# FFN input transposed by DMA, doubled scales spread by two DMAs, quantizing in place: one change to a planned four-stage kernel

## The chip, the cores and the metric

The kernel runs on one core of one Trainium2 chip. A core has TensorE (PE in the profile, its weight loads are PEld), VectorE (DVE), ScalarE (ACT), GpSimd (POOL) and SyncE (SP), which here only issues DMAs. Matmuls write to PSUM, eight banks of 128 x 512 floats; everything else lies in SBUF, 128 partitions wide. The metric is the device time of one execution in microseconds, given as the median of several runs.

## The reference

The input x is [4, 2048, 256], float32. Four residual stages follow each other; each normalizes x with a layer norm and adds its result to x.

```python
x = L0_attn_a_x
x = x + _L0_attn_a_ref(_layernorm(x, axis=-1), ...)
x = x + _L0_ffn_ref(_layernorm(x, axis=-1), w_gate, w_up, w_down)
x = x + _L0_attn_b_ref(_layernorm(x, axis=-1), ...)
x = x + _L0_ffn_ref(_layernorm(x, axis=-1), w_gate, w_up, w_down)
```

The first attention has a factor s / s, which it computes, and values v. The second is a linear attention over the first axis of x, which has 4 entries, with 16 heads of 16 and two gates. What the change touches is the FFN, which runs twice with the same weights. Its linear layers take both operands through a 4-bit grid, in blocks of 16 along the last axis:

```python
def fp4_quant_dequant(x):
    xb = x.reshape(shape[:-1] + (shape[-1] // BLOCK, BLOCK))
    scale = jnp.max(jnp.abs(xb), axis=-1, keepdims=True) / 6.0
    scale = jnp.maximum(scale, jnp.float32(1e-12))
    xn = xb / scale
    idx = jnp.searchsorted(_MID, jnp.abs(xn))
    q = _GRID[idx] * jnp.sign(xn) * scale
    return q.reshape(shape)

gate = fp4_linear(x, w_gate)      # x: 256 wide, w_gate and w_up: [704, 256]
y = fp4_linear(x, w_up)
h = jax.nn.silu(gate) * y
return fp4_linear(h, w_down)      # w_down: [256, 704]
```

So both the normalized input (256 wide, 16 blocks a row) and the hidden h (704 wide, 44 blocks a row) are put on the grid, one scale a block. For a matmul the contracted axis must lie on the partitions, so both have to be transposed.

## The kernel before

The rows of x are cut into 16 groups (`group(j)`) of 128 positions on the second axis times all 4 entries of the first (S = 4). A group is one tile x of [128, 4, 256], which stays in SBUF through all four stages: `attention_a`, `ffn_in` and four `ffn_tile` for k = 1, `attention_b`, and `ffn_in` and four `ffn_tile` for k = 2. That makes 32 inputs (`ffn_in`) and 128 hidden tiles (`ffn_tile`), of which the last four, of the last group in the second FFN, go a way of their own (`apart` is false). Before the groups, `first_pass` takes sums over the whole of x, and loads the weights and puts them on the grid (`quantize`, eight pieces).

Nothing is issued by hand in a loop's order. Every step is entered with `op(engine, us, rank, fn, reads, writes, ...)`: an engine, an assumed duration, a rank, and the buffers that it reads and writes. `land` is the time that a DMA is assumed to take after its issue, `port` marks steps that VectorE and GpSimd may not do at the same time, and `spare` says how many buffers of a pool must be left. `Plan.order` then plays the steps through with these costs: on each engine it takes the ready step with the lowest rank whose buffers are to be had. The program is written in the order that comes out. The ranks are offsets of a step in its stage plus the stage's begin, and the begins stand in the table `BEGIN`: one row a group, six numbers for attention a, the first input, its tiles, attention b, the second input, its tiles. Buffers come from pools of a few tiles each (`tiles(name, n, shape, ...)`); a step that needs one waits until the last user of one is done. Each engine, and SyncE's queue of DMAs, works strictly in the order written.

The path of one input (`ffn_in`):

1. GpSimd computes the reciprocal root of the variance (`root`), ScalarE normalizes four slices of x into xn (L384). Its blocks are 17 wide, the 17th element holds a small floor.
2. `to_grid`: VectorE takes the largest magnitude of each block (L1215) and its reciprocal (L1225) into the three rows of sx, divides by the scales into qax (L390); ScalarE takes magnitudes times 2^22 into qmx, in bfloat16 (L396); VectorE adds the larger of that and a floor (L403) and subtracts it again (L406), which rounds to the grid's steps. qax then holds the grid values, in float32.
3. `times_scales`: ScalarE divides the maxima by 6 (L1270), GpSimd multiplies qax by the scales (L1278).
4. `turn`: TensorE transposes qax in two banks of four 128 x 128 pieces (L1152), ScalarE copies each bank into one of six tiles of the pool turned (L1159).

The path of one hidden tile (`ffn_tile`): TensorE multiplies turned with gate and up weights in two halves (L1455), ScalarE takes the silu (L1476), VectorE the product h (L1487). `to_grid` follows, with h, qa, qm and sh as buffers, but its last pass writes grid values in bfloat16 to qm (128 x 768, the last 64 columns are zero). `scales_turned` transposes the 44 maxima of each row on TensorE (L1294), ScalarE divides by 6 into sT (L1302), and six DMAs, one for each chunk of 128 hidden features, write each scale's row 16 times to the partitions of its block, in the tile hqT (L1311): DMAs of 128 x 128, the last of 64 x 128. One DMA transposes qm to gT in six blocks (L1513). GpSimd multiplies hqT by gT (L1522), and TensorE multiplies with the down weights (L1559). VectorE adds to x (L342 or L1591). In the second FFN a DMA stores the rows (L1599).

The four tiles that are not apart take the way of the input: scales by `times_scales` on qa, transposes by TensorE (L1535), copies by ScalarE (L1548).

The other stages' matmuls are all in `project` (L1175), their transposes in `turn` too.

Of the kernel before, what the change touches and what calls it, by code (L numbers as in the profile page):

```python
# [14 lines left out]
ALU = mybir.AluOpType  # L15
# [241 lines left out]
def kernel(  # L257
# [79 lines left out]
    dev = one([P, D], "dev")  # L337
# [50 lines left out]
    def over_scales(a, src, rs):  # L388

        nc.vector.scalar_tensor_tensor(  # L390
            blocks(a), over_blocks(rs), -6.0 * BELOW, src, ALU.mult, ALU.mult
        )
# [30 lines left out]
    floored = tiles("xn", 1, [P, S * D // BLK, BLK + 1], fp)  # L423
    floored += tiles("h", 3, [P, FB, BLK + 1], fp)
    tiles("qax", 2, [P, S * D], fp)
    tiles("qmx", 1, [P, S * D], fp, BF16)
    tiles("sx", 2, [P, 3, S * D // BLK], fp)
    tiles("sil", 2, [P, HF], fp)
    tiles("qa", 3, [P, FF], fp)
# [5 lines left out]
    tiles("sT", 2, [FB, P], fp)  # L435
    tiles("sh", 4, [P, 3, FB], fp)
# [17 lines left out]
    def first_pass():  # L454
# [264 lines left out]
        def quantize(at, load, p, n):  # L719
            raw, a, m, w = (plan.buf(t) for t in ("hqT", "qa", "qm", "sh"))  # L720
# [6 lines left out]
            def sc(i):  # L727
                return w.ap[:p, i, :g]
# [22 lines left out]
                lambda: over_scales(ap(a), blocks(ap(raw)), sc(2)),  # L751
                [(raw, 0), (w, 0)],
                [(a, 0)],
# [6 lines left out]
                lambda: to_steps(ap(m), ap(a)),  # L760
                [(a, 0)],
                [(m, 0)],
            )
            for i, step in enumerate((to_sum, from_sum)):
# [4 lines left out]
                    lambda step=step: step(ap(a), ap(m)),  # L769
                    [(m, 0)],  # L770
                    [(a, 0)],
# [7 lines left out]
                    blocks(ap(a)), blocks(ap(a)), over_blocks(sc(1))  # L779
                ),  # L780
                [(w, 1)],
                [(a, 0)],
                port=True,
            )
            return a
# [3 lines left out]
        for i, chunks in enumerate(((0, 1), (2, 5), (6, 7), (3, 8), (4, 9), (10,))):  # L789
# [16 lines left out]
            def turn(a=a, tp=tp, n=n):  # L806
                for c in range(KC):
                    for t in range(n):
                        nc.tensor.transpose(
                            tp.ap[:, (n * c + t) * P : (n * c + t + 1) * P],  # L810
                            a.ap[:, t * D + c * P : t * D + (c + 1) * P],
# [15 lines left out]
        for i in range(2):  # L827
# [7 lines left out]
            for h in range(2):  # L835
                tp = plan.buf("bank")

                def turn(a=a, tp=tp, h=h):
                    for c in range(3):
# [3 lines left out]
                            tp.ap[:n, c * P : (c + 1) * P], a.ap[:, f : f + n], ident  # L843
# [131 lines left out]
        squares = plan.buf("qa")  # L975
# [133 lines left out]
        (-378, -314, -1376, -1348, 17, -996),  # L1109
        (-171, 99, -285, -130, -472, 322),  # L1110
        (122, 38, -748, 219, 388, -82),
        (158, 551, 236, -943, -736, 79),
        (122, 249, 41, 366, 26, 456),
        (302, -212, 210, 483, 172, 520),
        (311, -49, 469, 567, 672, 628),
        (524, -460, -821, 668, 512, 748),
        (519, 272, 567, 701, -1142, 842),
        (-796, 432, 635, -1, 85, -733),
        (591, 210, 709, 812, 491, 900),
        (587, -818, 708, 347, -832, 1075),  # L1120
        (669, 869, 776, 998, 617, 372),
        (704, 918, 497, 497, 654, 1040),
        (878, -478, 120, -465, -5, 1514),
        (799, 1104, 439, 1042, 488, 420),
    ]

    def group(j):
# [79 lines left out]
        def to_grid(at, src, parts, a, m, q, us, to=None):  # L1207

            v = blocks_of(src)
            n = us["n"]  # L1210
# [5 lines left out]
                    q.ap[:, 0, :], src.ap, AX.X, ALU.max, apply_absolute_value=True  # L1216
                ),
                [(src, i) for i in parts],
# [6 lines left out]
                lambda: nc.vector.reciprocal(q.ap[:, 2, :], q.ap[:, 0, :]),  # L1225
# [7 lines left out]
                lambda: over_scales(a.ap, v(), q.ap[:, 2, :]),  # L1233
                [(src, i) for i in parts] + [(q, 2)],
                [(a, 0)],
# [6 lines left out]
                lambda: to_steps(m.ap[:, :n], a.ap),  # L1242
                [(a, 0)],
# [6 lines left out]
                lambda: to_sum(a.ap, m.ap[:, :n]),  # L1250
                [(m, 0)],
                [(a, 0)],
# [5 lines left out]
                at + 4.1,  # L1258
                lambda: from_sum(a.ap, m.ap[:, :n], to and to.ap[:, :n]),
                [(a, 0), (m, 0)],  # L1260
                [(to or a, 0)],
                port=True,
            )

# [52 lines left out]
        def blocks_of(b):  # L1317
            return lambda: b.ap[:, :, :BLK]
# [575 lines left out]
```

## Time and profile before

| | |
|---|---|
| median of 3 runs | 1483.82 us (1482.01 to 1486.37) |
| the profiled execution's own time | 1483.54 us |
| its span, first to last instruction | 1481.7 us |
| TensorE, idle in the span | 44.9 us |
| VectorE, idle in the span | 137.7 us |
| ScalarE, GpSimd busy | 794.4, 769.7 us |
| DMA queue of SyncE | 220880 packets, 95.60 MB, 33.8% of 16 engines' span |
| mean clock granted to TensorE | 0.998 |

A row of the profile's groups reads: source line, engine, operation, output <- inputs (numbers of buffers left out), shapes, how many; then busy time in us and the mean of one in ns; then the idle time of the engine just before these instructions and what ended it. A row of waits reads: who waited <- for whom, us in total, times, longest. A row of the timeline reads: start, length in us, engine, line, operation, how many of them are put together, and in brackets the idle time before. SPq is SyncE's queue, where the length of a DMA is the time of its issue and not of its transfer. PE's matmuls overlap each other, so that the durations of single ones add up to more than the busy time.

### The profile page before, as it was taken

How to read it: one execution, taken by the hardware profiler on the slowest of the kernel's cores; microseconds unless marked ns; L12 is line 12 of the kernel's file. 1: busy time of each engine (PE TensorE's matmuls, PEld its weight loads, DVE VectorE, ACT ScalarE, POOL GpSimd, SP SyncE). 2: the span in 40 equal slices, each digit the busy share in tenths (PEclk: the TensorE clock that was granted, in tenths of full speed). 3: DMA queues.
4: the chain of work that ended last, by engine and by line, in shares of the span. 5: the costliest groups of instructions: out<-in, count | busy, mean ns of one | idle time of the engine just before them, and what ended most of it. 6: DMA issues, size and time to landing. Idle time of an engine off the chain costs nothing.

```text
span 1481.7 us, 19959 instructions
## 1 busy us (share of the span) xinstructions
PE 1436.8 (97%) x5742; PEld 998.8 (67%) x5742; DVE 1344.0 (91%) x2139; ACT 794.4 (54%) x1693; POOL 769.7 (52%) x787
## 2 busy tenths in 40 slices
PE   7989999999999999999999999999999999999998
PEld 6745667666767667676666666676677667676776
DVE  6799999999899999988997999988999898999995
ACT  6656557742674545544376455557525744546332
POOL 5344556534763646454644537556365654564532
PEclk9999999999999999999999999999999999999999
DMA  8402422124324334143432433231344134322451
GB/s 258 120 0 37 65 44 38 35 51 81 61 45 83 65 63 79 36 86 55 89 74 34 65 58 68 46 67 27 60 96 78 38 62 74 63 56 40 92 90 40
DMA packets 220990, 96.87 MB, mean 65 GB/s; under 512 B 108240, under 2 KB 220624, under 8 KB 220880
## 3 DMA queue, kind: packets, MB, share of 16 engines
q1 hardware_dynamic: 220880, 95.60, 33.8%
q8 instruction: 45, 0.74, 0.2%
q14 instruction: 65, 0.53, 0.1%
HBM read 18.09 MB, written 8.39 MB: 18 GB/s over the span
## 4 chain that ended last, share of the span: by engine, by line
PE 67%; DVE 13%; POOL 7%; DMA 5%; issue 4%; ACT 3%; SPq 1%; POOLq 0%; ACTq 0%; DVEq 0%
PE bank L1455 30%; PE bank L1175 17%; PE bank L1559 17%; PE bank L1152 3%; DMA gT<-qm 3%; POOL hqT L1522 2%; DVE qa L403 1%; DVE qm L406 1%; DVE pp L1666 1%; DVE h L1487 1%; DVE sh L1215 1%; DVE qa L390 1%; DVE x L342 1%; POOL norms_f L358 1%; PE bank L1294 1%
## 5 line engine op out<-in xcount | busy, mean ns | idle before, releaser
L1455 PE MATMUL bank<-wguT,turned 128*128 128x352 f32 x2048 | 634.2, 459 | 2.0 <-ACT sil L1476 2.0
L1455 PEld LDWEIGHTS bank<-wguT,turned 128*128 128x128 f32 x2048 | 380.4, 190 | 201.5 <-issue 11.8
L1522 POOL TENSOR_TENSOR hqT<-hqT,gT 128x768 f32<-128x768 f32 x124 | 228.8, 1849 | 258.6 <-DMA gT<-qm 117.4
L1559 PE MATMUL bank<-wdT,hqT 128*128 128x256 f32 x1536 | 350.9, 380 | 7.1 <-POOL hqT L1522 6.6
L1559 PEld LDWEIGHTS bank<-wdT,hqT 128*128 128x128 f32 x1536 | 288.7, 190 | 66.8 <-POOL hqT L1522 16.7
L1476 ACT ACTIVATE sil<-bank 128x352 f32<-128x352 f32 x256 | 115.7, 457 | 131.5 <-PE bank L1455 123.3
L396 ACT ACTIVATE qm<-qa 128x704 bf16<-128x704 f32 (+2 forms) x136 | 106.0, 780 | 96.9 <-DVE qa L390 74.6
L1487 DVE TENSOR_TENSOR h<-sil,bank 128x352 f32<-128x352 f32 x256 | 128.4, 506 | 29.6 <-ACT sil L1476 15.5
L1774 POOL TENSOR_TENSOR pp<-vg,sc 128x1024 f32<-128x1024 f32 x64 | 138.6, 2179 | 22.2 <-DVE tok L1795 20.1
L403 DVE SCALAR_TENSOR_TENSOR qa<-qm,qa 128x704 f32<-128x704 bf16 (+2 forms) x136 | 141.0, 1039 | 7.7 <-ACT qm L396 7.4
L390 DVE SCALAR_TENSOR_TENSOR qa<-sh,h 128x704 f32<-128x704 f32 x128 | 133.4, 1047 | 0.5
L406 DVE SCALAR_TENSOR_TENSOR qm<-qm,qa 128x704 bf16<-128x704 bf16 x124 | 126.8, 1025 | 0.2
L1175 PE MATMUL bank<-wvz,turned 128*128 128x512 f32 x256 | 119.8, 608 | 6.9 <-ACT turned L1159 3.5
L1175 PE MATMUL bank<-wqkB,turned 128*128 128x512 f32 x256 | 120.4, 593 | 1.8 <-ACT turned L1159 1.8
L1159 ACT COPY turned<-bank 128x512 f32<-128x512 f32 x160 | 87.5, 584 | 64.2 <-PE bank L1152 63.8
L1215 DVE TENSOR_REDUCE sh<-h 128x44 f32<-128x748 f32 x128 | 118.3, 924 | 2.0
L1278 POOL TENSOR_TENSOR qax<-qax,sx 128x1024 f32<-128x1024 f32 x32 | 68.1, 2128 | 90.2 <-DVE qax L406 73.8
L348 ACT ACTIVATE dev<-x,norms_f 128x256 f32<-128x256 f32 x128 | 64.7, 506 | 50.5 <-DVE x L342 48.1
L1175 PEld LDWEIGHTS bank<-wvz,turned 128*128 128x128 f32 x256 | 47.6, 193 | 56.9 <-issue 42.5
L1666 DVE TENSOR_TENSOR pp<-qk 128x1024 f32<-128x1024 f32 x64 | 83.2, 1312 | 0.6 <-ACT qk L1654 0.6
L1302 ACT ACTIVATE sT<-bank 44x128 f32<-44x128 f32 x124 | 32.8, 267 | 92.7 <-PE bank L1294 50.8
L384 ACT ACTIVATE xn<-x,norms_f 128x256 f32<-128x256 f32 x128 | 67.5, 593 | 21.3 <-POOL norms_f L378 18.2
(193 smaller groups left out, 2079.3 us busy)
## 6 DMA issues: line engine op xcount, KB each, us to landing
hqT<-sT SPq DMA_DIRECT2D x620, 64.0 KB
x<-in_L_attn_a_x_dram SPq DMA_DIRECT2D x23, 512.0 KB
out_dram<-x SPq DMA_DIRECT2D x64, 128.0 KB
hqT<-sT SPq DMA_DIRECT2D x124, 32.0 KB
gT<-qm SPq DMA_TRANSPOSE x124
hqT<-in_L_ffn_w_down_dram SPq DMA_DIRECT2D x2, 352.0 KB
hqT<-in_L_ffn_w_gate_dram SPq DMA_DIRECT2D x5, 128.0 KB
hqT<-in_L_ffn_w_up_dram SPq DMA_DIRECT2D x5, 128.0 KB
```

The lines of the kernel that those rows point to most:

```text
L390: nc.vector.scalar_tensor_tensor(blocks(a), over_blocks(rs), -6.0 * BELOW, src, ALU.mult, ALU.mult)
L396: nc.scalar.activation(m, a, AF.Abs, scale=UP)
L403: nc.vector.scalar_tensor_tensor(a, m, FLOOR, a, ALU.max, ALU.add)
L406: nc.vector.scalar_tensor_tensor(a if to is None else to, m, FLOOR, a, ALU.max, ALU.subtract)
L1175: nc.tensor.matmul(bank.ap[:, :n], lhs.ap[:, c, s * P : (s + 1) * P], w[:, c, :], start=(c == 0), stop=(c == KC - 1),)
L1215: lambda: nc.vector.tensor_reduce(q.ap[:, 0, :], src.ap, AX.X, ALU.max, apply_absolute_value=True),
L1455: nc.tensor.matmul(bank.ap[:, :HF], xqT.ap[:, c, s * P : (s + 1) * P], w[:, c, cols], start=(c == 0), stop=(c == KC - 1),)
L1476: lambda g=g, sil=sil: nc.scalar.activation(sil.ap, g.ap[:, :HF], AF.Silu),
L1487: lambda u=u, sil=sil, half=half: nc.vector.tensor_mul(h.ap[:, half * FB // 2 : (half + 1) * FB // 2, :BLK], blocks(sil.ap), blocks(u.ap[: ...
L1522: lambda: nc.gpsimd.tensor_mul(hqT.ap, hqT.ap, gT.ap),
L1559: nc.tensor.matmul(o.ap[:, :D], hqT.ap[:, i, :], wdT[:, i, :], start=(i == 0), stop=(i == 5),)
L1774: nc.gpsimd.tensor_mul(pv.ap.rearrange("p t (n e) -> p t n e", e=HD), vg.ap[:, :, :D].rearrange("p t (n e) -> p t n e", e=HD), over_blocks ...
```

## The change

1. The FFN input's grid is turned by DMA. `to_grid` for the input now writes its last pass in bfloat16 to qmx. A DMA transposes qmx in eight blocks to a new tile gTx; `scales_turned` spreads the scales straight into a tile of the pool turned, and GpSimd multiplies that by gTx in place. The transposes of qax on TensorE and the copies into turned are gone for the input.
2. Scales are doubled. ScalarE divides the maxima by 6 and writes each twice, side by side (88 columns for a hidden tile, filled up to 96; 128 for an input). TensorE transposes those, ScalarE copies the result in strips of 32 partitions into sT or sTx (three, or four for an input). Two DMAs then write each row to 8 partitions, three or four chunks at a time. hqT therefore holds the even chunks first and then the odd ones, and the products and matmuls that read it go by that order.
3. `to_grid` and `quantize` work in place: a, which was qa or qax, is gone, and the passes read and write h, xn or, for the weights, hqT. The pools qa and qax are gone; xn has 2 tiles instead of 1, h 5 instead of 3. The last four tiles take their grid values in a tile of the pool pp. The tile dev, which takes squares that nobody reads, becomes bfloat16.
4. Some steps claim their output's buffer earlier (the entries named "place"), and the table `BEGIN` has new numbers.

The diff, cut to its core; what is left out are the same replacements in `quantize`, in the way of the last four tiles, and the tables' other rows.

```diff
-    dev = one([P, D], "dev")
+    dev = one([P, D], "dev", dtype=BF16)
...
-    floored = tiles("xn", 1, [P, S * D // BLK, BLK + 1], fp)
-    floored += tiles("h", 3, [P, FB, BLK + 1], fp)
-    tiles("qax", 2, [P, S * D], fp)
+    floored = tiles("xn", 2, [P, S * D // BLK, BLK + 1], fp)
+    floored += tiles("h", 5, [P, FB, BLK + 1], fp)
...
-    tiles("qa", 3, [P, FF], fp)
...
-    tiles("sT", 2, [FB, P], fp)
-    tiles("sh", 4, [P, 3, FB], fp)
+    tiles("sT", 2, [32, 3, P], fp)
+    tiles("sTx", 1, [32, S, P], fp)
+    tiles("gTx", 1, [P, S * KC, P], fp, BF16)
+    for t in tiles("sh", 4, [P, 2 * FB + 96], fp):
+        nc.gpsimd.memset(t[:, FB : FB + 96], 0.0)
...
     BEGIN = [
-        (-378, -314, -1376, -1348, 17, -996),
-        (-171, 99, -285, -130, -472, 322),
+        (-1267, -1367, -565, -1453, -368, -660),
+        (-179, 118, -394, -861, -344, 323),
...
-                lambda: over_scales(a.ap, v(), q.ap[:, 2, :]),
-                [(src, i) for i in parts] + [(q, 2)],
-                [(a, 0)],
+                lambda: over_scales(v(), v(), q.ap[:, -nb:]),
+                [(q, 2)],
+                [(b, i) for i in parts],
...
-                lambda: from_sum(a.ap, m.ap[:, :n], to and to.ap[:, :n]),
-                [(a, 0), (m, 0)],
-                [(to or a, 0)],
+                lambda: from_sum(v(), mv(), blocks(to())),
+                [(b, i) for i in parts] + [(m, 0)],
+                [(us["into"], 0)],
...
-        def scales_turned(at, q, dst):
-            bank, sT = plan.buf("bank"), plan.buf("sT")
+        def scales_turned(at, q, nb, dst, with_it, sT, us, to, spare=None):
+            bank = plan.buf("bank")
+            n = -(-2 * nb // 32)
+
+            def sd():
+                return q.ap[:, nb : nb + 32 * n]
+
+            op(
+                "ACT",
+                0.15 + nb / 1400.0,
+                at - 0.5,
+                lambda: nc.scalar.mul(
+                    blocks(sd()[:, : 2 * nb], 2),
+                    over_blocks(q.ap[:, :nb], 2),
+                    1.0 / 6.0,
+                ),
+                [(q, 0)],
+                [(q, 1)],
+            )
             op(
                 "PE",
                 0.109,
                 at,
-                lambda: nc.tensor.transpose(bank.ap[:FB, :P], q.ap[:, 0, :], ident),
-                [(q, 0)],
-                [(bank, 0)],
-            )
-            op(
-                "ACT",
-                0.157,
-                at + 0.5,
-                lambda: nc.scalar.mul(sT.ap, bank.ap[:FB, :P], 1.0 / 6.0),
-                [(bank, 0)],
-                [(sT, 0)],
-            )
+                lambda: nc.tensor.transpose(bank.ap[: 32 * n, :P], sd(), ident),
+                [(q, 1)],
+                [(bank, 0), (sT, "place"), (with_it, "place")],
+            )
+            for i in range(n):
+                op(
+                    "ACT",
+                    0.157,
+                    at + 0.5 + 0.1 * i,
+                    lambda i=i: nc.scalar.copy(
+                        sT.ap[:, i, :], bank.ap[32 * i : 32 * i + 32, :P]
+                    ),
+                    [(bank, 0)],
+                    [(sT, i)],
+                )
 
             def spread():
-                for i, f in enumerate(HC):
-                    n = min(P, FF - f) // BLK
-                    src = sT.ap[f // BLK : f // BLK + n]
+                for c in range(2):
                     nc.sync.dma_start(
-                        dst.ap[: n * BLK, i, :], src.unsqueeze(1).to_broadcast([n, BLK, P])
-                    )
-
-            op("SP", 4.9, at + 1, spread, [(sT, 0)], [(dst, "scale")], land=2.7)
+                        to(c),
+                        sT.ap[16 * c : 16 * c + 16].unsqueeze(1).to_broadcast([16, 8, n, P]),
+                    )
+
+            op(
+                "SP",
+                1.4,
+                at + 1,
+                spread,
+                [(sT, i) for i in range(n)],
+                [(dst, "scale")],
+                land=us,
+                spare=spare,
+            )
...
         def ffn_in(at, k):
...
-            times_scales(at + 11, qa, sx, 1.93)
-            return turn(
-                at + 14, qa, [0], lambda: qa.ap.rearrange("p (s d) -> p s d", s=S)
-            )
+            dst, gT = plan.buf("turned"), plan.buf("gTx")
+            scales_turned(
+                at + 7,
+                sx,
+                nb,
+                dst,
+                qm,
+                plan.buf("sTx"),
+                2.7,
+                lambda c: dst.ap[:, c, :].rearrange("p (s n) -> p s n", n=P),
+                {"turned": 1},
+            )
+            op(
+                "SP",
+                1.8,
+                at + 11,
+                lambda: nc.sync.dma_start_transpose(gT.ap, qm.ap),
+                [(qm, 0)],
+                [(gT, 0), (dst, "place")],
+                land=2.3,
+            )
+
+            def scale_input():
+                t = dst.ap.rearrange("p c (s n) -> p s c n", n=P)
+                nc.gpsimd.tensor_mul(t, t, gT.ap.rearrange("p (s c) n -> p s c n", c=KC))
+
+            op(
+                "POOL",
+                1.93,
+                at + 13,
+                scale_input,
+                [(gT, 0), (dst, "scale")],
+                [(dst, 0), (dst, 1)],
+                port=True,
+            )
+            return dst
...
+            def by_chunk(b):
+                return b.ap.rearrange("p (c i) n -> p i c n", c=2)
...
-                    lambda: nc.gpsimd.tensor_mul(hqT.ap, hqT.ap, gT.ap),
+                    lambda: nc.gpsimd.tensor_mul(
+                        by_chunk(hqT), by_chunk(hqT), gT.ap.rearrange("p (i c) n -> p i c n", c=2)
+                    ),
...
-                        hqT.ap[:, i, :],
+                        hqT.ap[:, 3 * (i % 2) + i // 2, :],
```

## The prediction

> **What bounds the kernel now.** I read four views: the busy time of each engine over the span, the same in three stretches (up to the first gate/up matmul, up to the last, and the tail), the waits of TensorE, and the chain that ended last.
>
> ```profile
> PE 1436.8 (97%) x5742; PEld 998.8 (67%) x5742; DVE 1344.0 (91%) x2139; ACT 794.4 (54%) x1693; POOL 769.7 (52%) x787
> PE 67%; DVE 13%; POOL 7%; DMA 5%; issue 4%; ACT 3%; SPq 1%; POOLq 0%; ACTq 0%; DVEq 0%
> ```
>
> ```profile
> 0.00:118.80 118.80, 100.96 (x477) 72.27 (x478) 95.29 (x239) 70.64 (x153) 51.74 (x135) 0.99 0.41 118
> 118.80:1455.10 1336.30, 1315.02 (x5165) 909.31 (x5164) 1238.94 (x1884) 717.79 (x1525) 713.49 (x651) 1.00 0.34 61
> 1455.10:1481.70 26.60, 20.87 (x102) 17.18 (x101) 9.75 (x17) 5.99 (x16) 4.44 (x3) 1.00 0.10 35
> ```
>
> The columns of the second fence are the stretch, its length, and busy us (with instructions) of PE, PEld, DVE, ACT and POOL. TensorE idles 44.9 us in all: 17.8 before the first gate/up matmul, 21.3 in the 1336 us of the middle, 5.7 in the tail. So in the middle TensorE sets the time: 1 us less TensorE work there is close to 1 us less span, until another engine has no slack left. VectorE is next: it idles 1336.3 − 1238.9 = 97.4 us in the middle.
>
> ```profile
> PE bank L579 <- ACT vg L384: 8.2, 2, 7.3
> PE bank L1559 <- POOL hqT L1522: 6.6, 8, 1.6
> PE bank L1294 <- DVE sh L1215: 5.5, 7, 1.7
> PE bank L1175 <- ACT turned L1159: 5.3, 3, 3.3
> PE bank L1152 <- POOL qax L1278: 1.7, 2, 1.1
> ```
>
> Total us, times, longest. Nothing that TensorE waits for is large, so no removed wait can bring much; only removed TensorE work can.
>
> **The change, part by part.**
>
> *The 256 transposes of the FFN input leave TensorE.* Their rows, and one place where they run:
>
> ```profile
> L1152 PE MATMUL bank<-ident,qax 128*128 128x128 f32 x256 | 34.6, 275 | 1.7 <-POOL qax L1278 1.7
> L1294 PE MATMUL bank<-ident,sh 128*44 128x128 f32 x124 | 32.8, 274 | 6.5 <-DVE sh L1215 5.5 <-ACT turned L1159 0.5 <-DVE x L342 0.4
> L1294 PEld LDWEIGHTS bank<-ident,sh 128*44 128x44 f32 x124 | 12.6, 102 | 21.5 <-DVE sh L1215 6.7 <-issue 3.9 <-ACT turned L1159 2.9
> ```
>
> ```profile
> 586.57 1.09 PE L1152 MATMUL bank<-ident,qax 128*128 128x128 f32 x8 [1.15 <-POOL qax L1278]
> 587.50 0.27 PE L1294 MATMUL bank<-ident,sh 128*44 128x128 f32 x1
> 587.61 1.04 PE L1152 MATMUL bank<-ident,x 128*128 128x128 f32 x8
> ```
>
> The 275 ns of one contain the pipeline's latency. What TensorE pays is the distance between starts: the eight of one input begin at 586.57, the next instruction at 587.50, so 0.93 us for eight, 0.116 each. 32 inputs × 0.93 = 29.8 us go. The busy sum of 34.6 is the other end, were the latency never overlapped. I take 29.8, since neighbours nearly always overlap.
>
> *New on TensorE:* 32 transposes of the doubled input scales (128 columns), at 0.116 each 3.7 us (8.7 at 273 ns). The 124 transposes of the hidden scales turn 96 columns and not 44: the loading of 44 columns took 102 ns, of 128 it took 141 ns, the moving side stays 128 wide. So 0 to 39 ns each, 0 to 4.8 us; I take the middle, 2.4. TensorE net: −29.8 + 3.7 + 2.4 = −23.7 us (between −16 and −31).
>
> *ScalarE:* 64 copies of 128x512 (584 ns, 37.4 us) and 32 small multiplications (254 ns, 8.1 us) go. New are 124 doublings of 128x88 and 32 of 128x128, near the 254 ns of the 128x64 form, so 0.25 to 0.35 each; and 372 + 128 copies of 32x128 instead of 124 of 44x128 (267 ns). That adds 156 × 0.3 + 376 × 0.27 = 148, net +103 us: 794 to about 895, 62% of the span. It lies beside TensorE; the cover is ScalarE's idle 46%. Where it is felt is behind silu: VectorE waited 15.5 us for silu, and three short copies in front of one silu are 0.8 us.
>
> *SyncE's queue:* 744 spread DMAs (median 699 ns of issue) become 312 of three or four times the size. No row shows their issue. The load of 128x4x256 has more rows and took 424 to 545 ns, the small spread 557 to 699; in proportion to size it would be 2.1 to 2.8 us. By the first, 312 × 0.7 = 218 us against 520 before; by the last some 700. I take the first. Added are 32 transposing DMAs of 8 blocks against the 1.31 us of 6 blocks, so 1.3 to 1.75 each, 42 to 56 us. The queue is in order, and it is felt now:
>
> ```profile
> 1109.53 9.29 SPq L1311 DMA_DIRECT2D hqT<-sT  x11
> 1114.37 1.68 DVE L406 SCALAR_TENSOR_TENSOR qm<-qm,qa 128x704 bf16<-128x704 bf16 x2
> 1118.91 1.76 SPq L1513 DMA_TRANSPOSE gT<-qm  x1
> 1123.01 1.65 POOL L1522 TENSOR_TENSOR hqT<-hqT,gT 128x768 f32<-128x768 f32 x1 [10.12 <-DMA gT<-qm]
> ```
>
> A grid done near 1115 is transposed at 1118.91, behind eleven spreads. Such delays end in TensorE's waits for hqT and in idle of the middle, at most 21.3 us. I credit 3 (0 to 8).
>
> *VectorE* keeps every instruction (1937 in both orders of instructions) and every size; only views change, from one buffer to another to in place with a step of 17. No row shows a price for the step as output alone, but the product L1487 already writes it: 506 ns for 352 elements from PSUM, and 880 ns (median) for 704 reading it in L390. I take 0; a loss of 3% of the 158 passes at 1.04 us would be 5 us per pass, under VectorE's 97 us of idle. *GpSimd:* the input's product of 128x1024 gets a bf16 factor: 1936 ns (median) before, by the 1648 ns for 768 elements of L1522 up to 2200, so 0 to +8 us beside 48% idle. *In place with more tiles:* two xn and five h let TensorE run further ahead; no wait in the view is for them, so nothing.
>
> *The input's new path.* Each of 32 inputs no longer goes product, transposes, copies (584.59 to 588.38 above, 3.8 us), but transposing DMA, product. From issue to the product the 6-block DMA took 3.8 us (1447.49 to 1451.25) to 5.9 (148.77 to 154.64); with the product of 2 us that is 6 to 8 us or, for 8 blocks, somewhat more: 2 to 5 us longer per input. What hides it is TensorE's other work. In the new order of instructions, priced by the rows above, between an input's scale transpose and its first gate/up matmul lies TensorE work of 6 us at least, 21 in the median; 8 of 32 have under 14. The chain takes some 6 to 8 us of passes (575.1 to 583.2 for one input), then 6 to 8, so 12 to 16. The first input cannot be hidden: its first gate/up matmul at 118.8 has only the chain before it. I add 3 us there (0 to 8). For the others 0.
>
> *New ranks* reorder everything. Counted by instructions, the work of TensorE ahead of the first gate/up matmul is 72 us against 76, and behind the last one 14 against 20; VectorE's share is the same at each point within 30 us. I take the idle of the middle as unchanged.
>
> **The sum.** The profiled execution took 1483.5 us with a span of 1481.7; the median of the runs is 1483.8, so the two stand for each other. 1483.5 − 23.7 − 3 + 3 = 1460 us.
>
> **A rule that speaks against it.** The trace grants TensorE a clock of 0.98 in the two hundreds where it idles most (93.2 and 94.9 of 100 us), and 1.00 elsewhere. The Trainium skill, "TensorE: Matmul & The Clock Gate", section "What's actually happening", says that an idle window of about 3.4 us halves the clock, until a busy window as long restores it. A kernel with less TensorE work has more such gaps; by the rule a gap costs about 1.7 us more, an estimate from that page, and at the eight tight inputs the sum would be up to 14 us worse, 1474. The row gives 2 us in each of the two hundreds, which are in the sum already. I go by the row.
>
> **The rivals.**
>
> *VectorE becomes the second bound.* Its busy time stays 1344; in a middle of 1336 − 24 = 1312 us it idles 73 instead of 97. If the two engines' mutual waits keep 85 to 97 us of VectorE idle, 12 to 24 us come back: 1472 to 1484. For it: 94% busy in the middle. Against: 15.2 + 9.1 + 10.6 us of its waits are for TensorE, which now comes earlier, and TensorE idles 1.6% with VectorE at 93%.
>
> *Slower: the input's DMA path comes late.* Place: the gate/up matmul after each input transpose. If the chain behind the scale transpose takes 16 us, the tight inputs of the order are short by 10+3+4+1+3+5+8+4+5+1 = 44 us, at 14 by 26, at 12 by 12. It decides from about 14 us on, if the scale transpose is run when its input is just ready; 16 us gives 1460 + 44 = 1504. For it: landing up to 5.9 us with 6 blocks, a rise in DMA load (share 0.34 now; by the issues' sizes the spreads grow from 44.7 to 65.5 MB and 8.4 MB are transposed in addition, on 95.6 MB). Against: the scale transpose often stands in TensorE's queue later than its input, so part of the chain is past by then.
>
> *The spreads get no cheaper to issue:* if it grows with their size, SyncE's queue stays as full as it is. The credit of 3 us goes and hqT comes later at some tiles: 1463 to 1475.
>
> **How the numbers follow.** No change and measurement differ by about 0.3%, 4.5 us. The sum as worked out (1448 to 1470): 0.64. Better, with much of the middle's idle gone too (under 1448): 0.06. VectorE or SyncE's queue takes a part (1470 to 1479): 0.13. All of it taken back (1479 to 1488): 0.06. Slower by the input's path: 0.11. Faster thus 0.83, same 0.06, slower 0.11. The range 1443 to 1480 leaves out the slower case, most of the same, and a little below.
>
> **What would show it.** Right: 5518 matmuls (5742 − 256 + 32), busy TensorE near 1413 us, idle 40 to 50; ScalarE near 895; VectorE within 15 us of 1344; a spread's issue under 1 us. Wrong: TensorE waits for GpSimd's product into turned with over 10 us in total, VectorE above 94% of the span, issue of the spreads above 1.5 us, or a first gate/up matmul later than 127 us.

## The result, and the profile after

The changed kernel takes 1538.46 us in the median (1533.61 to 1541.02, four runs) against 1484.82 (1482.01 to 1486.37, four runs): 1.036 times as long, with a 95% interval of 1.0327 to 1.0393. It is slower by 54 us where 24 us less were forecast. The profiled execution took 1536.62 us.

The first lines of the page of the changed kernel, busy time by engine, SyncE's queue (packets, MB, share of 16 engines' span) and the chain that ended last:

```profile
PE 1438.7 (94%) x5518; PEld 985.1 (64%) x5518; DVE 1355.7 (88%) x2139; ACT 883.3 (58%) x2125; POOL 755.9 (49%) x794
...
q1 hardware_dynamic: 206848, 124.83, 48.4%
...
PE 39%; DVE 26%; DMA 11%; POOL 8%; ACT 8%; issue 7%; SPq 1%; POOLq 0%; ACTq 0%; DVEq 0%
```

TensorE runs the 5518 matmuls that were forecast, 224 fewer than before, and is busy for longer all the same: 1438.7 us against 1436.8. Its idle time is 1534.8 − 1438.7 = 96.1 us where it was 44.9. Of the 76.6 us between forecast and profiled run, 51.2 are idle time and 25.7 are matmuls that took longer than the 1413 us forecast. TensorE is no longer most of the chain that ended last: 39% of it, where it was 67%.

The waits of TensorE, of GpSimd for its two products and of ScalarE for qm, in the changed kernel (us in total, times, longest):

```profile
POOL hqT L1619 <- DMA gT<-qm: 213.7, 47, 11.3
...
POOL turned L1507 <- DMA gTx<-qmx: 81.2, 16, 11.2
...
ACT qm L396 <- DMA gT<-qm: 41.3, 17, 4.1
...
PE bank L1660 <- POOL hqT L1619: 40.4, 28, 3.8
...
PE bank L1533 <- POOL turned L1507: 14.6, 9, 4.0
```

Before, the first and the third of these were

```profile
POOL hqT L1522 <- DMA gT<-qm: 117.4, 32, 10.1
...
ACT qm L396 <- DMA gT<-qm: 19.4, 18, 3.4
```

and the fourth was 6.6 us. In place of the fifth TensorE waited 1.7 us for the input's product qax. So TensorE's waits for products are 55.0 us where they were 8.3, which is most of the 51.2 us of added idle time. TensorE waits for products, and the products wait for the transposing DMA. The sizes and the median landing of the DMAs, from the issue of each, show what stands in front of it:

```profile
hqT<-sT SPq DMA_DIRECT2D x248, 192.0 KB, 4.2
turned<-sTx SPq DMA_DIRECT2D x64, 256.0 KB, 5.5
...
gT<-qm SPq DMA_TRANSPOSE x124, 3.1
```

One place in the timeline of the changed kernel, with the lines that follow from each other:

```profile
608.41 1.24 SPq L1610 DMA_TRANSPOSE gT<-qm  x1
...
616.00 1.20 SPq L1342 DMA_DIRECT2D hqT<-sT  x2
616.57 0.88 DVE L406 SCALAR_TENSOR_TENSOR qm<-qm,h 128x704 bf16<-128x704 bf16 x1
617.49 2.77 SPq L1610 DMA_TRANSPOSE gT<-qm  x1
...
623.87 0.79 ACT L396 ACTIVATE qm<-h 128x704 bf16<-128x704 f32 x1 [4.14 <-DMA gT<-qm]
623.94 1.64 POOL L1619 TENSOR_TENSOR hqT<-hqT,gT 128x768 f32<-128x768 f32 x1 [11.01 <-DMA gT<-qm]
624.69 1.64 DVE L403 SCALAR_TENSOR_TENSOR h<-qm,h 128x704 f32<-128x704 bf16 x1 [2.98 <-ACT qm L396]
625.63 4.54 PE L1660 MATMUL bank<-wdT,hqT 128*128 128x256 f32 x12 [3.85 <-POOL hqT L1619]
```

The pair of spreads is issued in 1.20 us. The grid is ready at 617.45 and its transposing DMA is issued at once. At 608.41, with nothing ahead of it, such an issue took 1.24 us; here, behind the pair, it takes 2.77. The product starts 6.45 us after the issue began, and TensorE has stood still for 3.85 us. ScalarE needs the same tile qm again and has lost 4.14 us, and VectorE behind it 2.98.

### The profile page after: what moved, and what is told of

It reads as the page before. It is cut to its first block, busy times and chain, and to the rows that moved or that the text cites. A ratio compares the mean times of both kernels' runs of the same rounds, so it can differ in the third digit from the quotient of the medians.

```text
span 1534.8 us, 18821 instructions
## 1 busy us (share of the span) xinstructions
PE 1438.7 (94%) x5518; PEld 985.1 (64%) x5518; DVE 1355.7 (88%) x2139; ACT 883.3 (58%) x2125; POOL 755.9 (49%) x794
## 3 DMA queue, kind: packets, MB, share of 16 engines
q1 hardware_dynamic: 206848, 124.83, 48.4%
## 4 chain that ended last, share of the span: by engine, by line
PE 39%; DVE 26%; DMA 11%; POOL 8%; ACT 8%; issue 7%; SPq 1%; POOLq 0%; ACTq 0%; DVEq 0%
PE bank L1533 18%; PE bank L1660 10%; PE bank L1176 9%; DMA gT<-qm 6%; DVE qm L406 2%; DVE h L390 2%; POOL hqT L1619 2%; DVE pp L1767 2%; DMA gTx<-qmx 2%; DVE sh L1223 2%; DVE sc L1774 2%; DVE h L1565 2%; DVE h L403 2%; DVE x L342 1%; POOL turned L1507 1%
## 5 line engine op out<-in xcount | busy, mean ns | idle before, releaser
L1533 PE MATMUL bank<-wguT,turned 128*128 128x352 f32 x2048 | 641.8, 464 | 19.5 <-POOL turned L1507 14.6
L1660 PE MATMUL bank<-wdT,hqT 128*128 128x256 f32 x1536 | 363.6, 389 | 41.7 <-POOL hqT L1619 40.4
L1619 POOL TENSOR_TENSOR hqT<-hqT,gT 128x768 f32<-128x768 f32 x124 | 222.9, 1799 | 308.1 <-DMA gT<-qm 213.7
L1660 PEld LDWEIGHTS bank<-wdT,hqT 128*128 128x128 f32 x1536 | 293.6, 194 | 113.8 <-POOL hqT L1619 60.8
L396 ACT ACTIVATE qm<-h 128x704 bf16<-128x704 f32 x128 | 100.6, 788 | 107.0 <-DVE h L390 57.0
L403 DVE SCALAR_TENSOR_TENSOR h<-qm,h 128x704 f32<-128x704 bf16 x128 | 136.8, 1073 | 24.9 <-ACT qm L396 24.6
L390 DVE SCALAR_TENSOR_TENSOR h<-sh,h 128x704 f32<-128x704 f32 x128 | 130.5, 1029 | 0.2
L1333 ACT COPY sT<-bank 32x128 f32<-32x128 f32 x372 | 94.6, 254 | 61.3 <-PE bank L1324 52.8
L406 DVE SCALAR_TENSOR_TENSOR qm<-qm,h 128x704 bf16<-128x704 bf16 x124 | 126.7, 1024 | 0.2
L1507 POOL TENSOR_TENSOR turned<-turned,gTx 128x1024 f32<-128x1024 f32 x32 | 74.1, 2317 | 103.2 <-DMA gTx<-qmx 81.2
L1312 ACT ACTIVATE sh<-sh 128x88 f32<-128x88 f32 x124 | 34.0, 274 | 99.1 <-DVE sh L1223 98.6
L348 ACT ACTIVATE dev<-x,norms_f 128x256 bf16<-128x256 f32 x128 | 64.8, 506 | 37.4 <-DVE x L342 35.1
```

The costliest lines, as they stand in the source:

```text
L390: nc.vector.scalar_tensor_tensor(a, over_blocks(rs), -6.0 * BELOW, src, ALU.mult, ALU.mult)
L403: nc.vector.scalar_tensor_tensor(a, m, FLOOR, a, ALU.max, ALU.add)
L406: nc.vector.scalar_tensor_tensor(a if to is None else to, m, FLOOR, a, ALU.max, ALU.subtract)
L1533: nc.tensor.matmul(bank.ap[:, :HF], xqT.ap[:, c, s * P : (s + 1) * P], w[:, c, cols], start=(c == 0), stop=(c == KC - 1),)
L1619: lambda: nc.gpsimd.tensor_mul(by_chunk(hqT), by_chunk(hqT), gT.ap.rearrange("p (i c) n -> p i c n", c=2)),
L1660: nc.tensor.matmul(o.ap[:, :D], hqT.ap[:, 3 * (i % 2) + i // 2, :], wdT[:, i, :], start=(i == 0), stop=(i == 5),)
```

## The experiments

Theory A, formed from these lines: the merged spreads are cheap to issue but land as a burst that the plan did not reckon with, and what stands behind them comes late. The plan allows 1.4 us of issue and 2.6 or 2.7 to land, so 4.0 or 4.1 from the first issue; the second DMA of a pair is issued 0.6 us after the first, so by these medians it lands after 0.6 + 4.2 = 4.8 and 0.6 + 5.5 = 6.1 (taken pair by pair from the trace, the medians are 5.1 and 6.7). A landing need not cost by being late in itself: before, the last packet of a hidden tile's six spreads was done 7.1 us after the first issue in the median, later than now, but the plan allowed 4.9 of issue and 2.7 to land, 7.6 in all. Its rivals: the new table `BEGIN` (B), the small steps on ScalarE and the passes in place (C, later E), the FFN input's own path, which was the forecast's slower rival (D).

### The table of ranks

```diff
     BEGIN = [
-        (-1267, -1367, -565, -1453, -368, -660),
+        (-378, -314, -1376, -1348, 17, -996),
...
```

> The changed kernel with the table BEGIN of the kernel before; nothing else differs, and the order is planned anew from it. Theory A (the two merged spreads arrive as a burst which lands later than the plan assumes and holds up the transposing DMA behind them): the new table is not the cause, and the old one, sought for other operations, leaves even less room; 1540 to 1580 us. Theory B (the new table is the mistake, an order too tight by itself): 1480 to 1505 us, most of the loss gone.

1620.32 us, 1.0896 (1.0874 to 1.0919). The old numbers are 82 us worse, beyond theory A's range too, and TensorE's idle time is 149.9 us. Theory B falls in this form: for the changed kernel the new table is better than the old one.

### Lighter spreads, and where

```diff
-                        to(c),
-                        sT.ap[16 * c : 16 * c + 16].unsqueeze(1).to_broadcast([16, 8, n, P]),
+                        to(c)[:, :1],
+                        sT.ap[16 * c : 16 * c + 16, :1].unsqueeze(1).to_broadcast([16, 8, 1, P]),
```

> The changed kernel in its own order, with the same number of DMAs, but each merged spread carries only the first of its three (hidden units) or four (FFN input) chunks of 128 numbers, 64 KB in packets of 512 B in place of 192 or 256 KB; the other chunks of the scales are left out, so the products use stale scales. Theory A (burst): the transposing DMA issues in about 1.3 us behind a spread where it took 2.8, TensorE's waits for GpSimd's products (40.4 + 14.6 us) go mostly, and the time falls by 35 to 60 us, to 1478 to 1503. Theory B (order) or theory C (more small copies on ScalarE, the bfloat16 quantizer in place): less than 15 us, 1523 to 1538.

> As the run with light spreads, but only the 32 spread pairs of the FFN input are light (64 in place of 256 KB a DMA); the 124 pairs of the hidden units are whole. Theory A: the input's share goes, at most the 14.6 us that TensorE waits for the turned input and a little of what follows; 1515 to 1530 us. Theory D (the FFN input's own path through the DMA queue is what costs, the rival of the forecast): most of the loss goes, 1480 to 1505 us.

> As the run with light spreads, but only the 124 spread pairs of the hidden units are light (64 in place of 192 KB a DMA); the 32 pairs of the FFN input are whole. Theory A: most of the loss goes, as TensorE's 40.4 us for the hidden units' product do; 1490 to 1515 us. Theory D (the input's path): under 15 us, 1523 to 1538.

(The second and third do the same for one kind of spread only. Where the hidden units are light, hqT is also cleared whole at the start. The chunks that are not sent hold zeros or old values.) All light: 1484.93 us, 0.9998 (0.9984 to 1.0013). Input alone light: 1524.06, 1.0247 (1.0227 to 1.0266). Hidden units alone: 1492.01, 1.0041 (1.0024 to 1.0058). With the same number of DMAs, the same order and every other instruction, a third or a quarter of the bytes takes away the whole loss, 53.5 us: 46.5 when it is done for the hidden units, 14.4 for the input. That is theory A, and D is a quarter of it. The waits of TensorE with light spreads:

```profile
PE bank L1660 <- POOL hqT L1619: 9.3, 9, 2.2
PE bank L580 <- ACT vg L384: 8.5, 2, 7.6
...
PE bank L1533 <- POOL turned L1507: 1.4, 1, 1.4
```

The 40.4 and 14.6 us are 9.3 and 1.4. The transposing DMA of hidden units issues in 1.25 us on average (1.79 in the changed kernel), and its last packet is done 2.36 us after the issue began (3.13). Against the kernel before, the difference is smaller: there it issued in 1.45 us and was done after 2.83 on average, and one in ten took more than 3.5 us, where in the changed kernel one in ten takes more than 4.5.

### Two chunks of three or four

```diff
-                        to(c),
-                        sT.ap[16 * c : 16 * c + 16].unsqueeze(1).to_broadcast([16, 8, n, P]),
+                        to(c)[:, :2],
+                        sT.ap[16 * c : 16 * c + 16, :2].unsqueeze(1).to_broadcast([16, 8, 2, P]),
```

> The changed kernel in its own order, each merged spread with two of its three or four chunks (128 KB a DMA), the others left out. Between one chunk (1484.9 us) and all (1538.5 us). If the loss goes with the bytes that stand before the transposing DMA, some half of the 53.6 us comes back: 1505 to 1515 us. If the plan has slack that covers a spread up to some length and only the rest costs, it is nearer to one chunk: 1486 to 1500 us. If what costs is any spread of more than one 512 B piece per packet, it is nearer to all: 1520 to 1538 us.

1478.14 us, 0.9957 (0.994 to 0.9973): a little below the kernel before, 60 us below the whole spreads, and below all three expected ranges, of which that of a slack in the plan is nearest. So the loss does not go with the bytes; there is an edge between two chunks and three. The page and the DMAs of this run:

```profile
PE 1421.6 (96%) x5518; PEld 978.5 (66%) x5518; DVE 1351.8 (92%) x2139; ACT 881.9 (60%) x2125; POOL 766.4 (52%) x794
```

```profile
hqT<-sT SPq DMA_DIRECT2D x248, 128.0 KB, 3.1
turned<-sTx SPq DMA_DIRECT2D x64, 128.0 KB, 3.1
...
gT<-qm SPq DMA_TRANSPOSE x124, 2.8
```

A pair now lands 0.6 + 3.1 = 3.7 us after the first issue, inside the 4.0 that the plan allows; with three chunks 4.8, outside. So I read it: what stays inside is covered by the order, what is outside goes through to TensorE. No run shows it directly, since none was planned with another landing time. That two chunks are 7 us faster than one was not expected by any theory. VectorE is busy for 1365.8 us with one chunk and 1351.8 with two, on the same instructions; why is open.

### In pieces, and from another queue

```diff
                 for c in range(2):
-                    nc.sync.dma_start(
-                        to(c),
-                        sT.ap[16 * c : 16 * c + 16].unsqueeze(1).to_broadcast([16, 8, n, P]),
-                    )
+                    for i in range(n):
+                        nc.sync.dma_start(
+                            to(c)[:, i : i + 1],
+                            sT.ap[16 * c : 16 * c + 16, i : i + 1]
+                            .unsqueeze(1)
+                            .to_broadcast([16, 8, 1, P]),
+                        )
```

> The changed kernel in its own order; each merged spread is issued in pieces of one chunk, 64 KB in packets of 512 B, so six DMAs a tile of hidden units and eight a tile of input in place of two, with the same bytes. Theory A1 (what costs is that 192 to 256 KB a DMA stand in the queue within 1.2 us): issuing takes some 6 x 0.6 = 3.6 and 8 x 0.6 = 4.8 us, the transposing DMA behind no longer waits for packets but is issued 2.4 to 3.6 us later, so the delay changes its form and not its size; 1525 to 1560 us. Theory A2 (what costs is the large packets: one of 1536 B took 159 ns and one of 2048 B 231 ns on average, one of 512 B before 44): the DMA engines' time for the spreads falls by up to 45% and with it most of the loss; 1485 to 1510 us.

1597.1 us, 1.0765 (1.0746 to 1.0784). The transposing DMA is no longer held (issue 1.27 us, last packet 2.50), but it comes to be issued later, and the spreads too arrive later. The waits of TensorE and GpSimd in this run:

```profile
PE bank L1663 <- POOL hqT L1622: 68.4, 36, 5.3
...
POOL hqT L1622 <- DMA hqT<-sT: 66.1, 13, 9.7
```

In the changed kernel these two waits (the lines are L1660 and L1619 there) were 40.4 and 27.1 us. The delay changes its form, as A1 said, and is larger than A1's 1560. A2 falls: the packets of 512 B are no cheaper together, they take 500 us of 16 engines against 433 for the large ones.

```diff
-                    nc.sync.dma_start(
+                    nc.scalar.dma_start(
                         to(c),
```

> The changed kernel in its own order; the merged spreads are issued by ScalarE, right behind its own copies of the scales, in place of SyncE, so the transposing DMA on SyncE's queue is behind no spread. Theory A3 (the transposing DMA is held by its place in the same queue): its issue takes about 1.25 us everywhere, TensorE's waits for GpSimd's products fall to about those with light spreads, and the time falls to 1490 to 1510 us, less what ScalarE's 156 x 1.2 = 187 us of issuing cost where it was 58% busy. Theory A4 (the 16 DMA engines themselves are taken by the spread's packets, whatever the queue): the transposes still land about 2 us late, and the time stays at 1525 to 1560 us.

1569.98 us, 1.059 (1.0563 to 1.0617). The transposing DMA, now alone with loads and stores on SyncE's queue, still issues in 1.68 us on average and ends after 3.26, one in ten after more than 5.3. TensorE still waits for the product:

```profile
PE bank L1660 <- POOL hqT L1619: 46.3, 35, 6.3
```

So it is not the place in one queue that holds it (A3); what is left of the two theories is that the same 16 engines do (A4). The time is above A4's range as well: the further 31 us appear with ScalarE's issuing, and were not taken apart.

### The late chunk behind the transposing DMA

Nothing is left out here; the bytes are only put elsewhere.

```diff
-            def spread():
+            def spread(i=0, k=2):
                 for c in range(2):
...
+            return lambda: spread(2, n)
...
-                    lambda: nc.sync.dma_start_transpose(gT.ap, qm.ap),
+                    lambda: (nc.sync.dma_start_transpose(gT.ap, qm.ap), rest()),
...
+                        for v in (slice(0, 2), slice(2, 3))
```

> The changed kernel in its own order, nothing left out: the merged spreads send two chunks (128 KB a DMA) where they were issued, and the third chunk (the third and fourth for the input) in two more DMAs right behind the transposing DMA, in the same step of SyncE's order; GpSimd's product is cut in two instructions, the second on the late chunks. Theory A (the bytes that stand in front of the transposing DMA cost, since TensorE waits for what lands behind them): the transposing DMA lands as with two chunks, the late pair lands about 1.24 + 0.6 + 2.4 = 4.2 us after the transposing DMA's issue, when the product's first part (some 1.2 us from a landing at 2.8) is just done; near the 1478 us of the run with two chunks, with the cost of 156 more GpSimd instructions and some collisions with the next tile's spreads: 1480 to 1505 us. Theory G (the DMA engines' total time, 433 us over 16 engines for the spreads where the kernel before had 241, costs wherever it stands): most of the loss stays, 1515 to 1540 us.

1497.68 us, 1.0079 (1.0056 to 1.0103). With all of its bytes the kernel gets back 41 of 54 us, for bytes moved from in front of the transposing DMA to behind it. Its page, and the waits that matter:

```profile
PE 1430.9 (96%) x5518; PEld 983.1 (66%) x5518; DVE 1331.8 (89%) x2139; ACT 881.1 (59%) x2125; POOL 814.7 (54%) x950
...
q1 hardware_dynamic: 251776, 124.85, 47.3%
```

```profile
POOL hqT L1625 <- DMA gT<-qm: 155.6, 41, 12.9
...
POOL hqT L1625 <- DMA hqT<-sT: 46.6, 33, 6.9
...
PE bank L1670 <- POOL hqT L1625: 11.0, 11, 2.7
```

The DMA engines are as busy as in the changed kernel (47.3% and 48.4%), so theory G, that their total time costs wherever it stands, falls. For most of the loss it is the position. Since no scale is left out here, the result does not hang on zeros or old values. Whether a product is late because its spread lands late or because its transposing DMA does, no run takes apart. It does not beat the kernel before: GpSimd's product in two instructions takes 266.7 us against 222.9, and it waits for spreads at 33 places (7 in the changed kernel).

### ScalarE's small copies

```diff
-                    lambda i=i: nc.scalar.copy(
-                        sT.ap[:, i, :], bank.ap[32 * i : 32 * i + 32, :P]
-                    ),
+                    lambda i=i: i == 0
+                    and nc.scalar.copy(sT.ap[:, i, :], bank.ap[32 * i : 32 * i + 32, :P]),
```

> As the run with light spreads (1484.9 us), and ScalarE copies only the one chunk of the doubled scales that is sent: 344 of its 500 small copies of 0.255 us are left out as well, 88 us of ScalarE. Theory E (with the burst gone, ScalarE's added small copies are what keeps the kernel from the 1460 us of the forecast): 1465 to 1478 us. Theory F (the remaining difference is TensorE's clock, 0.992 in place of 0.998, and waits of under 10 us at many places): under 6 us, 1479 to 1487.

1474.74 us, 0.9935 (0.9917 to 0.9953): 10.2 us less than light spreads with all copies. Theory E holds for that much, and F, which allowed under 6 us, does not explain it. The copies are not all hidden beside ScalarE's 41% of idle time. A spread waits for the last copy of its strips; whether that or ScalarE's time is what costs, this run does not say.

### Another order

```diff
     BEGIN = [
-        (-1267, -1367, -565, -1453, -368, -660),
+        (-920, -902, -1213, -3949, -1133, -820),
...
```

> The changed kernel with another table BEGIN, sought so that the planned order ends early when it is followed through with the durations of the profiles: the merged spreads landing 4.9 (hidden units) and 6.5 us (input) after the first issue in place of the planned 4.0 and 4.1, and a transposing DMA behind them waiting for them. Theory B (the change is sound and its table alone was sought for the wrong landing times): below the kernel before, 1460 to 1484 us. Theory A (the bytes of the merged spreads cost in any order): part comes back, as the order can put other work between, but not all; 1500 to 1530 us.

> The kernel before with a table BEGIN sought in the same way and for as long, with its own six spreads landing 7.5 us after the first issue: the measure for the run above, so that a new table is compared with a new table. Both theories: 1470 to 1485 us, a little below the 1484 of its own table.

1530.45 us, 1.0321 (1.0296 to 1.0346), and 1487.52 us, 1.0013 (0.9997 to 1.0028). A table sought for the real landings brings 6 (by the ratios) to 8 us to the changed kernel, and none to the kernel before. It is a weak test, since the way of seeking did not help even there: it says that no order was found that hides the burst, not that there is none. Only `BEGIN` was changed: the plan itself went on assuming that a spread lands after 2.6 or 2.7 us. What the changed kernel takes with the real landings put into the plan was not run, and it is the first thing left to try.

### Where the source lies

```diff
-                    lambda i=i: nc.scalar.copy(
-                        sT.ap[:, i, :], bank.ap[32 * i : 32 * i + 32, :P]
-                    ),
+                    lambda i=i: [
+                        nc.scalar.copy(
+                            sT.ap[p : p + 32, i, :], bank.ap[32 * i : 32 * i + 32, :P]
+                        )
+                        for p in (0, 64)
+                    ],
...
-                        sT.ap[16 * c : 16 * c + 16].unsqueeze(1).to_broadcast([16, 8, n, P]),
+                        sT.ap[80 * c : 80 * c + 16].unsqueeze(1).to_broadcast([16, 8, n, P]),
```

> The changed kernel in its own order, nothing left out; ScalarE copies every strip of doubled scales twice, to partitions 0 to 31 and to 64 to 95, and the second DMA of a pair reads its 16 rows from partitions 80 to 95 in place of 16 to 31. What it asks is why the spreads' packets are slow: one of 1024 B took 101 ns in the run with two chunks where the loads' packets of 1024 B, to 128 partitions, took 53. Theory H (the two DMAs of a pair read from neighbouring partitions and get in each other's way there): the packets of 1536 B fall from 159 ns to 110 or 130, the pair lands 0.5 to 1 us earlier, and 10 to 35 us come back, less what 500 more copies of 0.255 us on ScalarE cost (344 fewer brought 10 us): 1515 to 1545 us. Theory I (where the source lies does not matter): packets within 5% of 159 ns, and 500 more copies; 1545 to 1565 us.

1585.37 us, 1.0672 (1.0638 to 1.0706). The packets of 1536 B take 157.9 ns on average against 158.6: whether the second half of the source lies on partitions 16 to 31 or 80 to 95 does not matter, and theory H falls. The time missed both ranges. The pair lands as before, and the doubled copies

```profile
L1334 ACT COPY sT<-bank 32x128 f32<-32x128 f32 x744 | 189.6, 255 | 59.6 <-PE bank L1324 48.4
```

put three copies, 0.77 us, in front of each hidden tile's spreads (0.77 × 124 + 1.02 × 32 = 128 us in all), and the kernel is 47 us slower. It fits theory A that a delay in front of the spreads costs as a late landing does, but ScalarE's other work comes later too, and the two were not taken apart.

## Why the prediction was wrong, point by point

*The step that failed* is SyncE's queue: "I credit 3 (0 to 8)". The spreads were priced by their issue alone, and the issue was right: the forecast said 0.7 us each, the medians are 0.56 and 0.59. What had no term was their landing, and what is queued behind them. Before, six spreads were issued over about 4.7 us and their last packet was done 7.1 us after the first issue, within the 7.6 that the plan allowed. Issued in 1.2 us, a pair lands 5.1 or 6.7 us after its first issue, where the plan now allows 4.0 or 4.1, and a transposing DMA right behind it issues in 2.8 us in place of 1.24. In place of the credit of 3 us, this cost 53.5 us, by the run with light spreads. The forecast had the growth from 44.7 to 65.5 MB in its text, as an argument in a rival, and gave it no price.

*"I take the idle of the middle as unchanged"* followed from that: 96.1 us of idle time in all instead of 44.9.

*The TensorE term*, −23.7 us, was right in its work (5518 matmuls) and wrong in its time. Set beside each other, the profiled executions of the runs with 5518 matmuls show why:

| run | TensorE idle, us | TensorE busy, us | clock granted |
|---|---|---|---|
| light, one copy | 53.5 | 1418.4 | 0.995 |
| two chunks | 55.8 | 1421.6 | 0.994 |
| light | 61.5 | 1425.7 | 0.992 |
| hidden units light | 63.5 | 1425.3 | 0.993 |
| late chunk behind | 66.2 | 1430.9 | 0.989 |
| input light | 89.6 | 1434.2 | 0.989 |
| another order | 90.7 | 1436.1 | 0.985 |
| changed kernel | 96.1 | 1438.7 | 0.986 |
| spreads on ScalarE | 120.0 | 1448.4 | 0.986 |
| in pieces | 128.1 | 1467.2 | 0.967 |
| copies doubled | 128.9 | 1457.7 | 0.977 |
| old table | 149.9 | 1465.3 | 0.967 |

The work is the same in every row. From the first to the last, 96.4 us more idle time bring 46.9 us more busy time: each us that TensorE waits costs about half a us again (counted from the first row, 0.44 to 0.65 in the rows with more than 85 us of idle time). The clock as granted goes most of the way with it but does not tell all: with the spreads on ScalarE it is that of the changed kernel, and TensorE is busy for 9.7 us longer. The page of the Trainium skill that the forecast weighed against itself ("TensorE: Matmul & The Clock Gate", section "What's actually happening") speaks of a clock that is halved after an idle window, and the rows agree in their direction. "I go by the row" was the wrong choice: the row of before showed a kernel with few gaps. The stretch from 100 to 200 us of the changed kernel shows what more gaps do (columns as in the forecast, then clock, DMA share and GB/s):

```profile
100.00:200.00 100.00, 85.67 (x299) 55.33 (x298) 88.70 (x131) 59.33 (x149) 44.58 (x48) 0.93 0.50 74
...
400.00:500.00 100.00, 90.70 (x343) 62.37 (x342) 89.86 (x119) 60.20 (x143) 51.54 (x50) 0.98 0.64 92
```

*ScalarE* came out at 883.3 us busy (895 forecast). That its idle time covers this was wrong by about 10 us, by the run with light spreads and one copy.

*VectorE* is within 12 us of 1344, as said, and *GpSimd's* product of the input has a median of 2.13 us, inside the bound. *The input's new path* was charged 3 us at the start; the first gate/up matmul came at 115.26 us, 3.5 earlier than before, so that charge was wrong in sign.

*The rivals.* The slower one, the input's path, had the sign and a mark that it named: TensorE's wait for the product into turned is over 10 us (14.6). But its place carries 14.4 us of the loss and the hidden units, which it left out, carry 46.5. VectorE as second bound did not decide: it is 88% busy in the slow kernel and 92% in the run with two chunks, which is 60 us faster. That the spreads get no cheaper to issue did not happen.

*What was right behind it:* with two chunks a spread, and so with some scales left out, the kernel takes 1478 us, inside the forecast's range and faster than before. The 18 us that are missing there to 1460 are 10.9 of idle time (55.8 against 44.9) and 8.6 of slower matmuls (1421.6 against 1413).

## What to carry to other kernels

Price a DMA that is merged by when its last byte lands and by what is queued behind it, not by its issue: the small ones may have been spacing the engines' work. In a program whose order is written ahead, look up what landing time the plan assumed; here two chunks that stayed within it cost nothing, and with the third, which did not, the loss reached TensorE; that the plan's figure is what draws this line is a reading and was not tested. When a change adds gaps to TensorE, add about half of the gaps again for slower matmuls, by these runs, and if a transfer is late, try first to put the bytes that are needed last behind the one that is needed first.

## What the runs showed of the hardware

- A pair of spreads that reads 16 rows of SBUF eight times and writes 128 partitions is slow for its size: the mean packet took 61.6 ns for 512 B, about 101 for 1024 B (worked out from the run with two chunks by taking off the loads' packets at 53), 158.6 for 1536 B and 231.1 for 2048 B. From 1024 to 2048 B, twice the bytes, that is 2.3 times as long. Packets of 1024 B from the loads took 53 ns. Before, six smaller spreads had packets of 512 B at 44.2 ns, so that the spreads' total over 16 engines went from 241 to 433 us. The reason is open; moving half of the source to other partitions changed nothing (157.9 ns).
- A transposing DMA's issue depends on what the engines still have to do: 1.24 us with nothing ahead, 2.8 on average within half a us behind a pair, and 1.68 on average with the spreads on another queue.
- The same product of GpSimd, of 768 elements a partition, took 222.9 us in 124 instructions and 266.7 in 248: cutting one in two costs about 0.35 us.
